# A four-layer graph-attention kernel: preparation of the next steps regrouped, statistics moved earlier, and elu's minimum fused with its scaling

## The chip, the cores and the metric

The kernel runs on one core of one Trainium2 chip. The metric is the device time of one execution in microseconds (us). The engines are TensorE (PE in the profile; PEld is its weight load), VectorE (DVE), ScalarE (ACT), GpSimd (POOL) and SyncE (SP), which here only issues DMAs. Each engine works off its own queue in program order, so an instruction that waits holds up everything behind it on that engine.

## The reference

Sixteen graphs of 1024 nodes with 256 features share one adjacency matrix. Four graph-attention layers follow each other, each with a pre-norm and a residual:

```python
h = jnp.maximum(_layernorm(x, axis=-1), 0.0)
x = x + _L0_gnn_ref(h, adj, L0_gnn_W, L0_gnn_a)   # 4 heads of 64, elu
...
x = x + _L1_gnn_ref(h, adj, L1_gnn_W, L1_gnn_a)   # 1 head of 256, elu
...
x = x + _L2_gnn_ref(h, adj, L2_gnn_W, L2_gnn_a)   # 4 heads of 64, elu
...
x = x + _L3_gnn_ref(h, adj, L3_gnn_W, L3_gnn_a)   # 1 head of 256, relu
```

A layer projects (`q = h @ W`), forms `e[i, j] = leaky_relu(src[i] + dst[j])` for each head, masks it by the adjacency, takes the softmax over j, multiplies by q, and applies elu (`max(y, exp(min(y, 0)) - 1)`) or, in the last layer, relu. Everything is fp32.

## The kernel before

**Steps and slots.** One step is one layer of one graph; there are 64. Four graphs are in flight, and `order_of_steps` interleaves them so that in the long middle part a four-head step (layers 0 and 2) and a one-head step (layers 1 and 3) alternate. Step n has eight *slots*, 8n to 8n+7. In each slot TensorE aggregates one group (L336, matmuls at L348): in a four-head step half of the rows of one head, so that two slots share a head, with matmuls of 64 output columns; in a one-head step an eighth of the rows, with matmuls of 128 columns. ScalarE evicts the group (`y`, L363).

**Weights.** For each head DVE makes eight tiles `w` (L332) of 128x1024, one for each block of 128 source nodes, from a broadcast row `g` that ScalarE has put into PSUM (L327) out of a row that a DMA fetched (L321). A group reads all eight tiles of its head. There are `WBUFS = 18` buffers for these tiles. `emit_tiles` (L456) issues up to 6 tiles a slot in a four-head step and 3 in a one-head step, never more than 18 past the last head that is done. So a four-head step can start with 18 of its 32 tiles made; the nineteenth takes the place of a tile of its first head, which is free when the second group has read it.

**Preparation.** While step n-2 runs, the next steps are prepared in *pieces* (L209): `stats` (eight `bn_stats` on DVE, L221, then ten small POOL operations, L242 to L254), two `normalise` (four ScalarE activations each, L260), and for each half two `transpose` (four PE transposes and one ScalarE eviction each, L268 and L269) and four `project` (two matmuls and a ScalarE eviction each, L279 and L281). The last projection of a half adds two exponentials on ScalarE (L287, L289) and one product on POOL (L291). Then come `factors` (two activations, L297 and L298), `rows` (one transpose, an eviction and a DMA, L303 to L307, then the fetches of L321) and an empty piece that marks the step as prepared. Transposes and projections share two PSUM buffers (`ps_p`), so the third of them waits for ScalarE to have evicted the first.

The lists at L44 to L48 say in which slot, counted from 8(n-2), each piece of step n is issued: `ONE` for one-head steps, `FOUR` for four-head steps, `SOON` and `LATE` where a graph is not free in time. Slots below 0 lie in step n-3, those above 7 in step n-1. `prepare` (L433) issues what is due after the group of each slot. With `FOUR` and `ONE` as they stand, a four-head step of the middle part has PE pieces after seven of its eight groups: slots 0 and 1 with the end of a one-head step's preparation, 0 to 5 and 7 with a four-head step's own. I call a run of such work between two groups a *PE piece*.

**The end of a step.** `finish` (L365) runs in the first slots of the next step: `divide` (reciprocal, L380), `scaled` for each half (y times 1/sum, L386, and for elu `min(y, 0)` into `e`, L391), `exponential` (L395), `add` (`max(e - 1, y)` on DVE, L401, and the residual on POOL, L402; in the last layer one DVE operation, L404). In a four-head step's finish the first half of y is scaled on DVE, the second on POOL; both minima run on POOL. The list `at` (L414) gives the slots: 0, 0, 0, 0, 1, 1, 1 after a four-head step, 0, 0, 1, 1, 2, 2, 3 after a one-head step.

**Pairs.** In what follows a *pair* is a one-head step and the four-head step behind it. There are two kinds. In a *layer-1 pair* the one-head step is a layer 1, so that its elu is finished inside the four-head step; in a *layer-3 pair* it is a layer 3, and its relu, its stores and the load of a new graph are.

Of the kernel before, what the change touches and what calls it, by code (L numbers as in the profile page):

```python
# [30 lines left out]
ALU = mybir.AluOpType  # L31
# [3 lines left out]
P = 128  # L35
# [5 lines left out]

FOUR = (-4, -3, -2, -1, 0, 0, 1, 1, 2, 2, 3, 3, 4, 4, 5, 5, 6, 7, 7, 10)  # L44
ONE = (2, 2, 4, 4, 5, 5, 6, 6, 7, 7, 6, 6, 7, 7, 8, 8, 8, 9, 9, 11)
SOON = (0, 0, 1, 2, 3, 3, 4, 4, 5, 5, 5, 5, 6, 6, 7, 7, 8, 9, 9, 11)
FIRST = (-2, -2, -1, -1, 0, 0, 0, 0, 1, 1, 1, 1, 2, 2, 2, 2, 3, 3, 3, 5)
LATE = (0, 0, 1, 1, 2, 2, 3, 3, 3, 3, 3, 3, 4, 4, 4, 4, 5, 6, 6, 8)  # L48


LAYERS = [
# [8 lines left out]
def kernel(ctx: ExitStack, tc: tile.TileContext, x, adj, ws, avs, out):  # L60
    nc = tc.nc
# [3 lines left out]
    HALF = C // 2  # L65
# [34 lines left out]
    L = len(LAYERS)  # L100
    steps = order_of_steps(B, L)
# [107 lines left out]
    def preparation(n):  # L209

        b, l = steps[n]
        H, slope, _, _ = LAYERS[l]
        D = F // H
        st = state[n]

        def stats(half):
            if half == 0:
                st["bn"] = small.tile([P, C, 6], F32, name="bn")
            bn = st["bn"]
            for c in range(half * HALF, (half + 1) * HALF):  # L220
                nc.vector.bn_stats(bn[:, c, :], xs[b][:, c, :])  # L221
            if n == 0:
                q = slice(half * HALF, (half + 1) * HALF)
                if half == 1:
                    combine_end(slice(0, HALF), nc.vector)
                combine(q, nc.vector)
                if half == 1:
                    combine_end(q, nc.vector)
            elif half == 1:
                combine(slice(0, C), nc.gpsimd)  # L230
                combine_end(slice(0, C), nc.gpsimd)

# [23 lines left out]
        def normalise(half):  # L256
            xn = st["xn", half] = prep.tile([P, HALF, F], F32, name="xn")
            for q in range(HALF):
                c = half * HALF + q
                nc.scalar.activation(xn[:, q, :], xs[b][:, c, :], AF.Identity,  # L260
                                     bias=st["shift"][:, c:c + 1], scale=st["rstd"][:, c:c + 1])
# [44 lines left out]
            st["grow"] = dram.tile([H, C, P], F32, name="grow")  # L306
            nc.sync.dma_start(out=st["grow"].rearrange("h c i -> c h i"), in_=gT)  # L307

        out = [lambda: stats(0), lambda: stats(1), lambda: normalise(0), lambda: normalise(1)]
        for half in range(2):  # L310
            out += [lambda half=half, k=k: transpose(half, k) for k in range(K)]
            out += [lambda c=c: project(c) for c in range(half * HALF, (half + 1) * HALF)]
# [52 lines left out]
    def finish(n):  # L365

        b, l = steps[n]
        H = LAYERS[l][0]
        D = F // H
        st = state[n]  # L370

        def views(half):
            s = slice(half * HALF, (half + 1) * HALF)
            return (xs[b][:, s, :].rearrange("p c (h d) -> p (c h) d", h=H),
                    st["y"][:, s, :, 0:D].rearrange("p c h d -> p (c h) d"),
                    st["r"][:, s, :].rearrange("p c h -> p (c h)"))

        def divide():
            st["r"] = small.tile([P, C, H], F32, name="r")
            nc.vector.reciprocal(st["r"], st["y"][:, :, :, D])  # L380

        def scaled(half):
            xh, yh, r = views(half)

            engine = nc.vector if H > 1 and half == 0 else nc.gpsimd
            engine.tensor_tensor(yh, yh, r[:, :, None].to_broadcast([P, HALF * H, D]),  # L386
                                 op=ALU.mult)
            if l < L - 1:

                e = st["e", half] = prep.tile([P, HALF * H, D], F32, name="e")  # L390
                nc.gpsimd.tensor_scalar(e, yh, 0.0, -3.0e38, op0=ALU.min, op1=ALU.max)  # L391

        def exponential(half):
            if l < L - 1:
                nc.scalar.activation(st["e", half], st["e", half], AF.Exp)  # L395

        def add(half):
            xh, yh, r = views(half)
            if l < L - 1:
                e = st["e", half]  # L400
                nc.vector.scalar_tensor_tensor(e, e, -1.0, yh, op0=ALU.add, op1=ALU.max)  # L401
                nc.gpsimd.tensor_add(xh, xh, e)  # L402
# [12 lines left out]
        return list(zip(at, (divide, lambda: scaled(0), lambda: exponential(0), lambda: scaled(1),  # L415
                             lambda: exponential(1), lambda: add(0), lambda: add(1)))) + (
                    [(4, lambda: store(0)), (4, lambda: store(1))] if l == L - 1 else [])

# [55 lines left out]
    last, agenda_of = {}, []  # L474
    for n, (b, l) in enumerate(steps):

        free = 8 * (last[b % STREAMS] + 1) + (8 if l == 0 else 2) if b % STREAMS in last else -99
        last[b % STREAMS] = n
        start = 8 * (n - 2)
        kind = ONE if LAYERS[l][0] == 1 else SOON if n < 4 else FOUR  # L480
        if free > start + kind[0]:
            kind = LATE
            start = max(free, agenda_of[-1][0] + 5)
        agenda_of.append([start + k for k in kind] if n > 1 else FIRST)
        if n > 2:

            was = agenda_of[n - 1]
            assert agenda_of[n][2] >= was[4] and agenda_of[n][3] >= was[10]
    ending = []
    later = {}  # L490
    with tc.manual_schedule():
        blocks = [mask_rows(c) for c in range(C)]
        layer = [weight_columns(l) for l in range(L)]
        layer[0][0](nc.scalar)
        load(0, 2)
        load_weights(0)
        for c in range(C):
            blocks[c][0]()
        load(1)
        load_weights(1)  # L500
# [12 lines left out]

        for i in (0, 1, 2, 3):
            first[i]()
        layer[0][2]()
        first[4]()
        first[5]()
        layer[0][3]()
        sign(0)  # L520
        for i, c in ((6, 1), (8, 2), (10, 3), (12, 4), (14, 5)):
            first[i]()
            first[i + 1]()
            sign(c)
        for piece in first[16:]:
# [12 lines left out]
        blocks[6][4]()  # L538
        blocks[7][4]()
        prepare(-1)  # L540
        for i in range(2, STREAMS):
            load_weights(i)
            load(i)

        for l, at in ((1, 1), (2, 8 * 3 + 3), (3, 8 * 5 + 3)):
            for i, piece in zip((0, 1, 2, 8), layer[l]):
                later[at + i] = piece
        for n in range(len(steps)):
            for k, (h, i0, per) in enumerate(groups(n)):
# [52 lines left out]
```

## Time and profile before

| what | value |
|---|---|
| median of 3 runs | 2643.99 us (2643.78 to 2644.14) |
| the profiled execution | 2644.88 us |
| its span, first to last instruction | 2643.1 us |
| PE busy | 2543.8 us (96%), granted clock 0.992 |
| DVE busy | 1987.4 us (75%) |
| ACT busy | 1141.3 us (43%) |
| POOL busy | 1014.6 us (38%) |
| a layer-1 pair, from row transpose to row transpose (L303) | 80.47 us |
| a layer-3 pair, likewise | 79.7 us |

The span is what the engines' instructions cover; the execution's own time has 1.8 us around it. The timeline of an engine lists its instructions in order, equal ones merged: start, time until the last of them ends, engine, line, operation, output and inputs, count, and in brackets the idle time before it and what ended that. An fp32 matmul shows as two records. Since matmuls are pipelined, what a stretch of them costs is best read as the distance from its start to the next start.

### The profile page before, as it was taken

The numbers are of one execution on the slowest core, as the hardware profiler recorded it, in microseconds if no ns is written. First come the engines' busy times: TensorE is split into PE (matmuls) and PEld (weight loads), VectorE is DVE, ScalarE is ACT, GpSimd is POOL, SyncE is SP. The second block draws the span as 40 slices with busy tenths as digits, with TensorE's granted clock in tenths as the row PEclk, the third lists the DMA queues.
The fourth block names the chain that finished last, engine by engine and source line by source line (L and its number), as shares of the span: only waits on it lengthen the run. The fifth ranks groups of instructions, "written<-read, shape, count | busy, mean of one in ns | idle before, by whom it ended". The sixth has DMA issues, their size and how long they took to land.

```text
span 2643.1 us, 87745 instructions
## 1 busy us (share of the span) xinstructions
PE 2543.8 (96%) x40088; PEld 2252.3 (85%) x40088; DVE 1987.4 (75%) x2112; ACT 1141.3 (43%) x2502; POOL 1014.6 (38%) x1072
## 2 busy tenths in 40 slices
PE   6889999999999999999999999999999999999999
PEld 4778888888888888888888888888888888888888
DVE  7887667877877777777778777778778777777873
ACT  4443444444444344444344444444443444444341
POOL 2233454432343443533332544443433334444231
PEclk8999999999999999999999999999999999999999
DMA  4101011121111110111211111101112201101101
GB/s 176 51 26 42 10 42 34 42 74 54 62 50 58 42 35 18 42 42 66 74 58 58 42 34 42 42 27 58 50 58 74 74 16 36 42 34 42 51 18 56
DMA packets 36987, 128.98 MB, mean 49 GB/s; under 512 B 6278, under 2 KB 9094, under 8 KB 34696
## 3 DMA queue, kind: packets, MB, share of 16 engines
q1 hardware_dynamic: 36606, 123.36, 13.4%
q8 instruction: 314, 5.14, 0.8%
q14 instruction: 57, 0.47, 0.1%
q10 hardware_dynamic: 10, 0.00, 0.0%
HBM read 105.91 MB, written 17.43 MB: 47 GB/s over the span
## 4 chain that ended last, share of the span: by engine, by line
PE 88%; DVE 6%; ACT 4%; issue 1%; POOL 1%; DMA 0%; POOLq 0%; DVEq 0%
PE acc L348 67%; PE pp L279 16%; PE pp L268 5%; DVE w L332 4%; ACT xn L260 2%; ACT e L395 1%; DVE bn L221 1%; PE pp L303 0%; ACT y L363 0%; ACT whx L281 0%; DVE e L401 0%; POOL shift L254 0%; DVE mask L194 0%; POOL e L391 0%; DMA x<-in_x 0%
## 5 line engine op out<-in xcount | busy, mean ns | idle before, releaser
L348 PE MATMUL acc<-whx,w 128*64 128x65 f32 x36864 | 1924.4, 241 | 21.2 <-DVE w L332 14.8
L348 PEld LDWEIGHTS acc<-whx,w 128*64 128x64 f32 x36864 | 1753.6, 144 | 195.6 <-issue 58.7
L332 DVE SCALAR_TENSOR_TENSOR w<-g,rcol,mask 128x1024 f32<-128x1024 f32 x1280 | 1547.2, 1273 | 232.7 <-PE acc L348 146.7
L363 ACT ACTIVATE y<-acc 128x260 f32<-128x260 f32 (+1 forms) x504 | 193.7, 384 | 1059.4 <-PE acc L348 1059.4
L291 POOL TENSOR_TENSOR whx<-whx 128x1024 f32<-128x1024 f32 x128 | 256.5, 2004 | 834.9 <-ACT whx L289 783.4
L279 PE MATMUL pp<-wx,hT 128*128 128x264 f32 (+1 forms) x2048 | 514.0, 393 | 40.3 <-ACT whx L281 32.3
L279 PEld LDWEIGHTS pp<-wx,hT 128*128 128x128 f32 x2048 | 373.2, 190 | 118.5 <-ACT whx L281 43.1
L260 ACT ACTIVATE xn<-x,shift,rstd 128x256 f32<-128x256 f32 x512 | 261.7, 588 | 123.2 <-POOL shift L254 121.2
L281 ACT ACTIVATE whx<-pp 128x264 f32<-128x264 f32 (+1 forms) x512 | 194.0, 385 | 232.8 <-PE pp L279 232.5
L402 POOL TENSOR_TENSOR x<-x,e 128x1024 f32<-128x1024 f32 x96 | 227.7, 2373 | 141.8 <-DVE e L401 139.5
L401 DVE SCALAR_TENSOR_TENSOR e<-e,y 128x1024 f32<-128x1024 f32 x96 | 145.4, 1515 | 181.0 <-ACT e L395 181.0
L391 POOL TENSOR_SCALAR e<-y 128x1024 f32<-128x1024 f32 x96 | 127.2, 1325 | 205.7 <-DVE y L386 192.0
L221 DVE BATCH_NORM_STATS2 bn<-x 128x6 f32<-128x256 f32 x512 | 178.0, 409 | 33.2 <-POOL x L402 30.0
L386 POOL TENSOR_TENSOR y<-y,r 128x1024 f32<-128x1024 f32 x94 | 178.1, 1896 | 33.6 <-DVE r L380 33.6
L327 ACT ACTIVATE g<-gs 128x1024 f32<-128x1024 f32 x160 | 163.5, 1023 | 6.8 <-DVE w L332 6.2
L268 PE MATMUL pp<-ident,xn 128*128 128x128 f32 x1024 | 152.0, 281 | 13.8 <-ACT whx L281 5.9
L268 PEld LDWEIGHTS pp<-ident,xn 128*128 128x128 f32 x1024 | 117.1, 142 | 44.9 <-ACT whx L281 23.2
L269 ACT ACTIVATE hT<-pp 128x512 f32<-128x512 f32 x256 | 141.0, 588 | 10.5 <-PE pp L268 5.4
L242 POOL TENSOR_TENSOR dev<-bn 128x8 f32<-128x8 f32 x63 | 13.2, 209 | 334.2 <-DVE bn L221 334.2
L380 DVE RECIPROCAL r<-y 128x32 f32<-128x32 f32 (+1 forms) x63 | 17.6, 279 | 158.8 <-ACT y L363 158.8
L248 POOL TENSOR_TENSOR rstd<-rstd,neghalf 128x8 f32<-128x8 f32 (+1 forms) x65 | 107.0, 1647 | 12.5 <-DVE shift L249 7.6
L395 ACT ACTIVATE e<-e 128x1024 f32<-128x1024 f32 x96 | 100.7, 1049 | 18.6 <-POOL e L391 18.6
(63 smaller groups left out, 436.7 us busy)
## 6 DMA issues: line engine op xcount, KB each, us to landing
gs<-grow SPq DMA_DIRECT2D x160, 512.0 KB
x<-in_x SPq DMA_DIRECT2D x15, 1024.0 KB
out<-x SPq DMA_DIRECT2D x30, 512.0 KB
w<-in_adj SPq DMA_DIRECT2D x8, 512.0 KB
x<-in_x SPq DMA_DIRECT2D x2, 512.0 KB
wx<-in_L_gnn_W SPq DMA_DIRECT2D x8, 128.0 KB
out<-x SPq DMA_DIRECT2D x8, 128.0 KB
grow<-gT SPq DMA_DIRECT2D x32, 16.0 KB
```

What stands on the lines that cost most here:

```text
L221: nc.vector.bn_stats(bn[:, c, :], xs[b][:, c, :])
L260: nc.scalar.activation(xn[:, q, :], xs[b][:, c, :], AF.Identity, bias=st["shift"][:, c:c + 1], scale=st["rstd"][:, c:c + 1])
L268: nc.tensor.transpose(pt[:, q, :], st["xn", half][:, q, k * P:(k + 1) * P], ident)
L279: nc.tensor.matmul(pw, lhsT=st["hT", half][:, k, q * P:(q + 1) * P], rhs=wx[l][:, k, :], start=(k == 0), stop=(k == K - 1))
L281: nc.scalar.activation(st["whx"][:, c, :], pw, AF.Copy)
L291: nc.gpsimd.tensor_tensor(wh[:, :, :, 0:D], wh[:, :, :, 0:D], wh[:, :, :, D:D + 1].to_broadcast([P, HALF, H, D]), op=ALU.mult)
L327: nc.scalar.activation(g, state[n]["gs", h], AF.Copy)
L332: nc.vector.scalar_tensor_tensor(w, state[n]["g", h], state[n]["rcol"][:, jc, h:h + 1], masks[LAYERS[steps[n][1]][3]][:, jc, :], op0=ALU.m ...
L348: nc.tensor.matmul(acc[o % P:o % P + cols, q, :], lhsT=st["w", h, jc][:, o:o + cols], rhs=st["whx"][:, jc, h * (D + 1):(h + 1) * (D + 1)], ...
L363: nc.scalar.activation(st["y"][:, i0:i0 + per, h, :], acc, AF.Copy)
L386: engine.tensor_tensor(yh, yh, r[:, :, None].to_broadcast([P, HALF * H, D]), op=ALU.mult)
L402: nc.gpsimd.tensor_add(xh, xh, e)
```

## The change

It has four parts.

- **Order of the preparation.** In a four-head step of the middle part only slots 0 and 2 are followed by PE pieces. Slot 0 takes the last four projections of a one-head step (before: two in the slot ahead and two here) together with the first four projections and the second pair of transposes of the next four-head step; slot 2 takes the row transpose of the one-head step and the last four projections of that four-head step. The first pair of transposes goes to the last slot of the one-head step ahead, and the row transpose to slot 0 of the one-head step behind.
- **Statistics.** The small POOL operations become a piece of their own (`combine_all`). Both `stats` pieces of a four-head step move to slot 0 of the one-head step ahead (from its slots 4 and 5), the combination to slot 3, and the two `normalise` to slots 5 and 6 (from 6 and 7).
- **elu after a four-head step.** DVE computes `e = min(y, 0) * r` in one operation for both halves, and POOL does both products `y * r`. Before, DVE did one product, POOL the other and the two minima. After a one-head step the operations stay as they were.
- **Bookkeeping.** `scaled(1)` is issued ahead of `exponential(0)`; a late preparation may start up to three slots earlier, which makes steps 7 and 9 `LATE` and changes the start of step 60; steps are entered into the agenda one ahead.

```diff
-FOUR = (-4, -3, -2, -1, 0, 0, 1, 1, 2, 2, 3, 3, 4, 4, 5, 5, 6, 7, 7, 10)
-ONE = (2, 2, 4, 4, 5, 5, 6, 6, 7, 7, 6, 6, 7, 7, 8, 8, 8, 9, 9, 11)
...
+FOUR = (-8, -8, -5, -3, -2, -1, -1, 0, 0, 0, 0, 0, 0, 2, 2, 2, 2, 3, 8, 8, 10)
+ONE = (2, 2, 2, 4, 4, 5, 5, 6, 6, 6, 6, 6, 6, 8, 8, 8, 8, 8, 10, 10, 12)
...
+LATE = (0, 0, 0, 1, 1, 2, 2, 3, 3, 3, 3, 3, 3, 4, 4, 4, 4, 5, 6, 6, 8)
...
-            elif half == 1:
+
+        def combine_all():
+            if n > 0:
                 combine(slice(0, C), nc.gpsimd)
                 combine_end(slice(0, C), nc.gpsimd)
...
-        out = [lambda: stats(0), lambda: stats(1), lambda: normalise(0), lambda: normalise(1)]
+        out = [lambda: stats(0), lambda: stats(1), combine_all, lambda: normalise(0), lambda: normalise(1)]
...
         def scaled(half):
             xh, yh, r = views(half)
-
-            engine = nc.vector if H > 1 and half == 0 else nc.gpsimd
-            engine.tensor_tensor(yh, yh, r[:, :, None].to_broadcast([P, HALF * H, D]),
-                                 op=ALU.mult)
+            rb = r[:, :, None].to_broadcast([P, HALF * H, D])
             if l < L - 1:
 
                 e = st["e", half] = prep.tile([P, HALF * H, D], F32, name="e")
+                if H > 1:
+                    nc.vector.scalar_tensor_tensor(e, yh, 0.0, rb, op0=ALU.min, op1=ALU.mult)
+            nc.gpsimd.tensor_tensor(yh, yh, rb, op=ALU.mult)
+            if l < L - 1 and H == 1:
                 nc.gpsimd.tensor_scalar(e, yh, 0.0, -3.0e38, op0=ALU.min, op1=ALU.max)
...
-        return list(zip(at, (divide, lambda: scaled(0), lambda: exponential(0), lambda: scaled(1),
+        return list(zip(at, (divide, lambda: scaled(0), lambda: scaled(1), lambda: exponential(0),
                              lambda: exponential(1), lambda: add(0), lambda: add(1)))) + (
...
-            start = max(free, agenda_of[-1][0] + 5)
+            start = max(free, agenda_of[-1][0] + 5, start - LATE[7])
...
-                while planned < len(steps) and agenda_of[planned][0] <= 8 * n + k:
+                while planned < len(steps) and min(
+                        a[0] for a in agenda_of[planned:planned + 2]) <= 8 * n + k:
```

More of the change, by code (lines that the diff above doesn't have):

```diff
@@ L39 @@
 WBUFS = 18
-FOUR = (-4, -3, -2, -1, 0, 0, 1, 1, 2, 2, 3, 3, 4, 4, 5, 5, 6, 7, 7, 10)
-ONE = (2, 2, 4, 4, 5, 5, 6, 6, 7, 7, 6, 6, 7, 7, 8, 8, 8, 9, 9, 11)
-SOON = (0, 0, 1, 2, 3, 3, 4, 4, 5, 5, 5, 5, 6, 6, 7, 7, 8, 9, 9, 11)
-FIRST = (-2, -2, -1, -1, 0, 0, 0, 0, 1, 1, 1, 1, 2, 2, 2, 2, 3, 3, 3, 5)
-LATE = (0, 0, 1, 1, 2, 2, 3, 3, 3, 3, 3, 3, 4, 4, 4, 4, 5, 6, 6, 8)
+FOUR = (-8, -8, -5, -3, -2, -1, -1, 0, 0, 0, 0, 0, 0, 2, 2, 2, 2, 3, 8, 8, 10)
+ONE = (2, 2, 2, 4, 4, 5, 5, 6, 6, 6, 6, 6, 6, 8, 8, 8, 8, 8, 10, 10, 12)
+SOON = (0, 0, 0, 1, 2, 3, 3, 4, 4, 5, 5, 5, 5, 6, 6, 7, 7, 8, 9, 9, 11)
+FIRST = (-2, -2, -2, -1, -1, 0, 0, 0, 0, 1, 1, 1, 1, 2, 2, 2, 2, 3, 3, 3, 5)
+LATE = (0, 0, 0, 1, 1, 2, 2, 3, 3, 3, 3, 3, 3, 4, 4, 4, 4, 5, 6, 6, 8)
 LAYERS = [
@@ L482 @@
             kind = LATE
-            start = max(free, agenda_of[-1][0] + 5)
+            start = max(free, agenda_of[-1][0] + 5, start - LATE[7])
         agenda_of.append([start + k for k in kind] if n > 1 else FIRST)
         if n > 2:
+            assert agenda_of[n][7] >= 8 * (n - 2)
             was = agenda_of[n - 1]
-            assert agenda_of[n][2] >= was[4] and agenda_of[n][3] >= was[10]
+            assert agenda_of[n][3] >= was[5] and agenda_of[n][4] >= was[11]
     ending = []
@@ L512, in sign @@
                 blocks[c - 1][3]()
-        for i in (0, 1, 2, 3):
+        for i in (0, 1, 3, 4):
             first[i]()
         layer[0][2]()
-        first[4]()
         first[5]()
+        first[6]()
         layer[0][3]()
         sign(0)
-        for i, c in ((6, 1), (8, 2), (10, 3), (12, 4), (14, 5)):
+        for i, c in ((7, 1), (9, 2), (11, 3), (13, 4), (15, 5)):
             first[i]()
@@ L524 @@
             sign(c)
-        for piece in first[16:]:
+        for piece in first[17:]:
             piece()
```

## The prediction

> **What bounds it now.** I read the page first, then the timelines of PE, DVE, ACT and POOL over one pair in the middle (1055 to 1137 us), then the distances between row transposes over the whole span. The page's chain of work that ended last is PE:
>
> ```profile
> PE 88%; DVE 6%; ACT 4%; issue 1%; POOL 1%; DMA 0%; POOLq 0%; DVEq 0%
> ```
>
> DVE, busy for 75%, is second, so the question is what PE loses and whether DVE lets it have that back. PE at the end of the one-head step and in the four-head step behind it:
>
> ```profile
> 1086.99 1.91 PE L279 MATMUL pp<-wx,hT 128*128 128x258 f32 x8
> 1090.17 2.01 PE L279 MATMUL pp<-wx,hT 128*128 128x258 f32 x8 [1.27 <-ACT whx L281]
> 1092.11 3.95 PE L348 MATMUL acc<-whx,w 128*64 128x65 f32 x128
> 1095.99 2.01 PE L279 MATMUL pp<-wx,hT 128*128 128x258 f32 x8
> 1097.84 1.29 PE L268 MATMUL pp<-ident,xn 128*128 128x128 f32 x8
> 1099.07 3.95 PE L348 MATMUL acc<-whx,w 128*64 128x65 f32 x128
> ...
> 1109.57 2.05 PE L279 MATMUL pp<-wx,hT 128*128 128x264 f32 x8
> 1111.55 3.95 PE L348 MATMUL acc<-whx,w 128*64 128x65 f32 x128
> ...
> 1128.17 7.69 PE L348 MATMUL acc<-whx,w 128*64 128x65 f32 x256
> 1135.79 0.28 PE L303 MATMUL pp<-ident,gcol 128*32 128x128 f32 x1
> ```
>
> One group alone takes 3.88 us (1092.11 to 1095.99), two in a row 7.62 (1128.17 to 1135.79): 3.74 each and 0.14 for each uninterrupted block. Two projections take 1.98 here (1109.57 to 1111.55) and 1.74 in the one-head step (1080.64 to 1082.38; at 264 columns 1.78 by width), so a piece costs another 0.20. Each interruption of the 64-column work thus costs 0.34 us. The bracket is a stall: ScalarE's `xn` for the four-head step began only at 1087.51, after 3.19 us of waiting for POOL's `shift`, and the eviction behind it was late. The Trainium skill, "TensorEngine Tiling (Array Packing)", section Key Properties, says that a change of tiling mode drains TensorE; it gives no price, the 0.34 is this trace's.
>
> DVE in the same four-head step:
>
> ```profile
> 1102.25 7.24 DVE L332 SCALAR_TENSOR_TENSOR w<-g,rcol,mask 128x1024 f32<-128x1024 f32 x6 [4.26 <-PE acc L348]
> 1109.41 1.22 DVE L401 SCALAR_TENSOR_TENSOR e<-e,y 128x1024 f32<-128x1024 f32 x1
> 1110.54 2.47 DVE L332 SCALAR_TENSOR_TENSOR w<-g,rcol,mask 128x1024 f32<-128x1024 f32 x2
> 1112.93 1.24 DVE L401 SCALAR_TENSOR_TENSOR e<-e,y 128x1024 f32<-128x1024 f32 x1
> 1114.73 9.63 DVE L332 SCALAR_TENSOR_TENSOR w<-g,rcol,mask 128x1024 f32<-128x1024 f32 x8 [0.56 <-PE acc L348]
> 1125.49 7.24 DVE L332 SCALAR_TENSOR_TENSOR w<-g,rcol,mask 128x1024 f32<-128x1024 f32 x6 [1.14 <-PE acc L348]
> 1136.33 0.35 DVE L380 RECIPROCAL r<-y 128x32 f32<-128x32 f32 x1 [3.59 <-ACT y L363]
> ```
>
> It stands idle until the second group frees the first buffers (4.26 us), then makes 22 tiles and two adds, is done at 1132.7, and waits 3.59 us for the step to end. Those 3.59 us are what the change will draw on.
>
> **Part 1, PE alone.** Four-head step now 43.80 us (1092.11 to 1135.91), seven blocks. After: three blocks, 8 x 3.74 + 3 x 0.14 = 30.34. Piece after slot 0: today's (two projections and transposes, 1095.99 to 1099.07) 3.08, two more projections 1.74, four of 264 columns 3.56, and a new stall of 0.33: between the last one-head projection and the next there are four small activations on ScalarE, which take 1.49 us from eviction to eviction today (1098.04 to 1099.53), so the third of the following projections finds its PSUM buffer free 2.11 us after they begin instead of 1.78. Sum 8.71. Piece after slot 2: today's row transpose and two projections with their stall, 2.73 (1102.95 to 1105.68), and 1.78: 4.51; in a layer-3 pair, without the exponential ahead of it, 1.99 (1183.41 to 1185.40) and 1.78: 3.77. The step is 43.56 or 42.82. One-head step now 36.67 (1055.44 to 1092.11). After: eight groups at 3.475 (20.85 for six) 27.80, rows 0.12, first transposes 0.87, four projections and transposes 2.88 + 1.74 = 4.62, the moved transposes 1.02 (as 1115.43 to 1116.45): 34.43. The stall of 1.27, with 0.17 around it, goes: the statistics come five slots earlier, so `shift` is no longer what `xn` waits for. A pair falls from 80.47 to 77.99, or from 79.72 to 77.25: **2.48 us each**.
>
> **Part 2, what DVE returns.** Times from the start of the new four-head step. Its second group begins at 3.88 + 8.71 = 12.59, not 6.96; the first buffer is free 3.18 later as today (1099.07 to 1102.25), at 15.77. With all 18 buffers full, DVE can do nothing earlier; its two adds stand behind six of the waiting tiles. Six tiles at 1.195 to 22.93, add 1.13, two tiles to 26.45, add to 27.6; the next buffers come free 3.18 after the fourth group's start (24.72), at 27.90; fourteen tiles to 44.63. The step ends at 43.56: DVE is **1.07 us late** into the one-head step. In a layer-3 pair the second add meets POOL's `whx` product (about 25.3 to 27.2) and ends at 28.2, so DVE is done at 44.93 against 42.82: **2.11 late**. The tiles themselves still arrive: the first one-head group needs its eighth 3.04 us after its start. But the elu chain stands behind them on DVE.
>
> The chain in the one-head step, from the moment D at which DVE is free: reciprocal 0.38, two fused minima at 1.14, eight `bn_stats` of the other graph 2.62 (today they come later): D+5.28. The nearest row for a fused minimum is L386's 1.23 us product with the same broadcast; L401's contended 2.06 bounds it above. POOL's two products (1.90 each) begin when the second minimum ends its reading and hold until D+6.4. Then the first add; it and the second end by D+8.5, POOL's two x adds (2.36 each) at D+13.3; statistics of the second half and the combination 1.48 and 4.22 (1068.48 to 1069.96 to 1074.18): `xn` starts at D+18.95. From `xn` to the next group are 2.82 us at least (140.31 to 143.13, where PE waits for each `xn`). So the seventh group starts at D+21.77; by PE alone it would at 0.12 + 20.85 + 0.87 = 21.84. Today it starts at 21.72 with `xn` at 18.74: the chain has 0.16 to spare, hence the loss is about D: 1.0 and 2.0 us.
>
> That DVE and POOL exclude each other is seen here:
>
> ```profile
> 1062.57 2.36 POOL L402 TENSOR_TENSOR x<-x,e 128x1024 f32<-128x1024 f32 x1
> ```
> ```profile
> 1063.95 2.06 DVE L401 SCALAR_TENSOR_TENSOR e<-e,y 128x1024 f32<-128x1024 f32 x1 [2.25 <-ACT e L395]
> ```
>
> The add took 2.06 instead of 1.23 us, ending about 1.07 after POOL did. `bn_stats` beside the same kind of POOL operation is not slowed (four in 1.39). The skill agrees ("SBUF — State Buffer", section SBUF: two separate sides: an exclusive lock for the whole instruction, held by whoever starts first). A rule that speaks against moving the minima is in "GPSIMD Engine Reference", section Engine selection: one-input operations run at roughly line rate on GpSimd. Here POOL's minimum took 1.04 us, less than the 1.23 that DVE pays; by that rule alone the move only loads DVE, 1.14 us a pair, which is inside the chain above.
>
> **Other parts.** POOL loses 2 x 1.04 us and gains 1.90 a pair, neither on a path but the chain's. SP: the rows DMA of a four-head step moves one slot back, behind group and exponential, some 5 us later; today's fetches were issued 3 us after it (1055.99, 1057.85) and the first `g` is not wanted before 10.9 us: hidden; uncovered it would hold ScalarE about 1 us. Stores and load in a layer-3 pair follow the adds, about 3 us later; the load landed about 13 us before the step's end: hidden. The `at` order and the DVE minimum let ScalarE's first exponential go about 1.2 us sooner in the four-head steps at the start (it waited 7.78 and 6.06 us for POOL `e` there), while DVE, which bounds those, gets 1.14 more in four places: -2.4 to +4.6, taken as 0. Steps 7, 9, 60 (`LATE`) and the pairs before 414 and after 2417 us keep more pieces: -3 to +3, taken as 0.
>
> **Sum.** From 414.5 to 2417.25 us there are 25 pairs, 13 with 80.47 and 12 with 79.7. 13 x (2.48 - 1.0) + 12 x (2.48 - 2.0) = 19.2 + 5.8 = 25.0. The span falls from 2643.1 to 2618.1; the execution has 1.8 more, and was 0.9 above the median, so against the median: 2643.99 - 25.0 = **2619.0**.
>
> **Rivals.**
> 1. The chain doesn't bind: DVE gets through sooner, or POOL's products come between other work. For it: 1 us is little against a chain of 22 us. Against: 22 tiles and two adds from 15.77 can't end before 44.3. The price is Part 1 whole, 25 x 2.48 = 62: 2582.
> 2. Everything is given back. If POOL takes the port between the two minima (its product is ready just as DVE turns to the second), the second ends 1.9 later and the chain is 0.95 longer: 25 x 0.95 = 24, giving 2643. Also here: the pieces are as they say, but 0.34 is an artefact of modelled matmul ends.
> 3. **Slower:** PE waits for `w`. Place: first group of the one-head step. Price: one us per us beyond D = 3.04, on top of a chain that then stalls by 3. At D = 4 a pair loses 4.0 - 2.48 = 1.5: 2644 + 38 = 2682; the change turns slower from D = 2.5 on. Fused minima at 2.06 and port losses of both adds would bring 1 to 2 us. Against: the first minimum finds POOL idle.
>
> **Chances.** Forecast 0.54 (2605 to 2636), rival 1 0.19, rival 2 0.14, rival 3 0.13. Leaving out the slow rival, the range is 2578 to 2646; the forecast's own is 2605 to 2636. A measurement of this kernel tells about 0.2% (5 us) from no change: faster 0.73, same 0.14, slower 0.13.
>
> **What would show it.** Right: two PE pieces in a four-head step, pairs of about 79.0 and 79.2 us, no 1.27 stall, DVE idle some 9.5 us ahead of the nineteenth tile, reciprocal 1 to 2 us after the step's end, PE transposes waiting for `xn` at slot 5 of the one-head step. Wrong: no such wait and pairs of 77 to 78; or PE idle behind `w`.

## The result, and the profile after

The changed kernel takes 2641.12 us (median of 4 runs, 2640.89 to 2642.87) beside 2643.93 for the kernel before (4 runs): a ratio of 0.9991, 95% interval 0.9973 to 1.0008. That is no difference that this measurement can tell. I had forecast 2619.0, with a range of 2578 to 2646 in all and of 2605 to 2636 for the forecast's own mechanism. The profiled execution took 2640.99, its span is 2639.2 us.

On the page after, DVE is busy for 77% (75), ACT and POOL hardly changed. The line of the chain that ended last answers to the first line shown of before, where PE had 88% and DVE 6%:

```profile
PE 66%; DVE 17%; POOL 7%; ACT 6%; issue 3%; DMA 0%; DVEq 0%; ACTq 0%
```

So PE now waits for chains on other engines in much of the span. PE's timeline of the changed kernel, at the end of a one-head step (layer 1) and in the four-head step behind it, answers to the rows of before:

```profile
1081.09 0.76 PE L271 MATMUL pp<-ident,xn 128*128 128x128 f32 x5 [0.17 <-ACT xn L263]
...
1098.11 5.54 PE L282 MATMUL pp<-wx,hT 128*128 128x258 f32 x24
...
1106.93 7.69 PE L351 MATMUL acc<-whx,w 128*64 128x65 f32 x256
1114.55 0.27 PE L306 MATMUL pp<-ident,gcol 128*8 128x128 f32 x1
...
1119.06 21.25 PE L351 MATMUL acc<-whx,w 128*64 128x65 f32 x650
```

There are two PE pieces, as forecast: 8.82 us from 1098.11 to 1106.93 (forecast 8.71) and 4.51 from 1114.55 to 1119.06 (forecast 4.51). The stall of 1.27 is gone; in its place the transposes ahead of 1081.69 wait for `xn` (1.92 us from 1079.77, where they took 0.87 before). DVE over the same stretch:

```profile
1059.76 0.34 DVE L383 RECIPROCAL r<-y 128x32 f32<-128x32 f32 x1
1060.21 2.36 DVE L392 SCALAR_TENSOR_TENSOR e<-y,r 128x1024 f32<-128x1024 f32 x2
...
1110.11 7.24 DVE L335 SCALAR_TENSOR_TENSOR w<-g,rcol,mask 128x1024 f32<-128x1024 f32 x6 [9.99 <-PE acc L351]
...
1122.24 16.78 DVE L335 SCALAR_TENSOR_TENSOR w<-g,rcol,mask 128x1024 f32<-128x1024 f32 x14 [0.21 <-PE acc L351]
1138.94 0.34 DVE L383 RECIPROCAL r<-y 128x32 f32<-128x32 f32 x1
```

The idle time ahead of the nineteenth tile is 9.99 us (4.26 before). After it DVE never pauses for more than 0.21 us (the rows left out are two tiles and the two adds, without a wait), and it is late: the reciprocal, which had waited 3.59 us, now waits for nothing and starts 0.94 us after the step's last eviction of `y` began (1058.82). In the kernel before it was 0.42 us, the eviction itself taking 0.39. All this is as forecast. The pairs are 79.18 us (80.47 before) in layer 1 and 79.06 (79.7) in layer 3; forecast were 79.0 and 79.2.

The loss lies elsewhere. A ruler that shows it is the start of each step's last `y` eviction; its distances are the steps' lengths (us, from the profiled executions):

| steps | before | after |
|---|---|---|
| 0 to 5, sum to the end of 5 | 334.45 | 328.00 |
| 6 (one head) | 33.74 | 40.39 |
| 7 | 46.42 | 45.11 |
| 8 (one head) | 34.05 | 46.82 |
| 9 to 55, sum | 1888.23 | 1865.85 |
| 56 to 59, sum | 157.69 | 161.68 |
| 60 (four heads) | 46.24 | 50.78 |
| 61 and 62, sum | 70.22 | 68.70 |

The pairs in the middle gain 22.4 us and the start 6.45. Steps 6 to 8 give 18.1 back, steps 56 to 60 give 8.5. This is step 8 of the changed kernel, on DVE, then on ScalarE, then on PE (the last `y` eviction of step 7 began at 413.50):

```profile
414.85 7.24 DVE L335 SCALAR_TENSOR_TENSOR w<-g,rcol,mask 128x1024 f32<-128x1024 f32 x6 [1.38 <-ACT g L330]
422.01 0.34 DVE L383 RECIPROCAL r<-y 128x32 f32<-128x32 f32 x1
```
```profile
443.52 4.04 ACT L263 ACTIVATE xn<-x,shift,rstd 128x256 f32<-128x256 f32 x8 [10.78 <-POOL shift L257]
```
```profile
444.18 2.81 PE L271 MATMUL pp<-ident,xn 128*128 128x128 f32 x8 [8.38 <-ACT xn L263]
```

Six tiles `w` of step 9 stand on DVE ahead of the reciprocal that ends step 7. Here the reciprocal comes 8.5 us after the eviction began; in the kernel before it came 0.42 us after it (414.62):

```profile
415.04 0.35 DVE L380 RECIPROCAL r<-y 128x32 f32<-128x32 f32 x1 [3.59 <-ACT y L363]
```

The elu, the statistics and `xn` follow it, and PE stands idle for 8.38 us. That is not the whole loss of 12.8 us in this step. Late in the idle time the granted clock fell to half, and the eight transposes took 2.59 us (0.87 before), the group behind them 5.26 (3.48 before). This row of a table of stretches shows the transposes; its figures are the stretch, its length, busy time and count of PE, PEld, DVE, ACT and POOL, PE's clock, the DMA engines' busy share and GB/s:

```profile
444.00:446.70 2.70, 2.48 (x8) 1.60 (x9) 0.00 (x0) 2.70 (x7) 2.36 (x5) 0.50 0.00 0
```

The code says why. With `FOUR` beginning at -8 the graphs of steps 7, 9 and 60 are not free in time, so their lists become `LATE`, which no step of the kernel before used. (Ahead of the prediction I put this down to late preparations being allowed an earlier start; that only moves the start of step 60.) The last number of a list is the empty piece that marks a step as prepared, and only then may `emit_tiles` go on to its tiles. `FOUR` sets the mark at 10 (slot 2 of step n-1), behind `finish`. `LATE` sets it at 8 from its start, which for steps 7 and 9 is slot 7 of step n-2: the tiles of step 9 are issued before the `finish` of step 7.

### The profile page after: what moved, and what is told of

It reads as the page before. It is cut to its first block, busy times and chain, and to the rows that moved or that the text cites. A ratio compares the mean times of both kernels' runs of the same rounds, so it can differ in the third digit from the quotient of the medians.

```text
span 2639.2 us, 87794 instructions
## 1 busy us (share of the span) xinstructions
PE 2539.8 (96%) x40088; PEld 2256.5 (86%) x40088; DVE 2041.7 (77%) x2144; ACT 1133.4 (43%) x2502; POOL 1021.5 (39%) x1040
## 3 DMA queue, kind: packets, MB, share of 16 engines
q1 hardware_dynamic: 36606, 123.36, 13.3%
q8 instruction: 314, 5.14, 0.8%
## 4 chain that ended last, share of the span: by engine, by line
PE 66%; DVE 17%; POOL 7%; ACT 6%; issue 3%; DMA 0%; DVEq 0%; ACTq 0%
PE acc L351 46%; PE pp L282 15%; DVE w L335 10%; PE pp L271 4%; POOL x L406 3%; DVE e L405 3%; DVE bn L222 2%; ACT xn L263 2%; POOL rstd L251 2%; ACT e L399 1%; DVE e L392 1%; ACT whx L284 1%; ACT rcol L290 0%; ACT gcol L301 0%; ACT whx L292 0%
## 5 line engine op out<-in xcount | busy, mean ns | idle before, releaser
L282 PE MATMUL pp<-wx,hT 128*128 128x264 f32 (+1 forms) x2048 | 488.6, 390 | 18.8 <-ACT whx L284 11.2
L393 POOL TENSOR_TENSOR y<-y,r 128x1024 f32<-128x1024 f32 x126 | 264.3, 2108 | 618.7 <-DVE e L392 490.8
L282 PEld LDWEIGHTS pp<-wx,hT 128*128 128x128 f32 x2048 | 379.6, 191 | 98.7 <-ACT whx L284 23.5
L406 POOL TENSOR_TENSOR x<-x,e 128x1024 f32<-128x1024 f32 x96 | 238.1, 2486 | 161.0 <-DVE e L405 155.5
L405 DVE SCALAR_TENSOR_TENSOR e<-e,y 128x1024 f32<-128x1024 f32 x96 | 175.6, 1839 | 41.7 <-ACT e L399 35.5
L271 PE MATMUL pp<-ident,xn 128*128 128x128 f32 x1024 | 168.6, 284 | 32.1 <-ACT xn L263 28.4
L392 DVE SCALAR_TENSOR_TENSOR e<-y,r 128x1024 f32<-128x1024 f32 x64 | 75.5, 1221 | 2.2
L408 DVE SCALAR_TENSOR_TENSOR x<-y,x 128x1024 f32<-128x1024 f32 x30 | 43.3, 1444 | 10.0 <-POOL y L393 10.0
```

Source lines behind the costliest of these rows:

```text
L271: nc.tensor.transpose(pt[:, q, :], st["xn", half][:, q, k * P:(k + 1) * P], ident)
L282: nc.tensor.matmul(pw, lhsT=st["hT", half][:, k, q * P:(q + 1) * P], rhs=wx[l][:, k, :], start=(k == 0), stop=(k == K - 1))
L393: nc.gpsimd.tensor_tensor(yh, yh, rb, op=ALU.mult)
```

## Experiments

Theory A: the pairs do what was forecast, and the early mark of `LATE` eats the gain. Rivals: the lateness of those pieces themselves, or the new elu operations, everywhere a little. Each series was timed beside the kernel before on its own chip (2644.38 to 2645.66 us there, so times of different series compare to about 2 us); ratios are to that, with 95% intervals.

**1. The mark alone.** Only the last number of `LATE` differs from the changed kernel.

```diff
-LATE = (0, 0, 0, 1, 1, 2, 2, 3, 3, 3, 3, 3, 3, 4, 4, 4, 4, 5, 6, 6, 8)
+LATE = (0, 0, 0, 1, 1, 2, 2, 3, 3, 3, 3, 3, 3, 4, 4, 4, 4, 5, 6, 6, 11)
```

> The changed kernel with one number different: the last, empty piece of LATE, which marks a step as prepared, moves from 8 to 11, where FOUR has it; all other pieces stay. Theory A (in steps 6 and 8 the early mark of steps 7 and 9 lets DVE issue six weight tiles of the next four-head step ahead of the elu of the step just ended, so that normalisation starts late and PE waits for xn): step 8 falls from 46.8 to about 35 us and step 6 from 40.4 to about 35, time about 2624 us. Rival B (LATE puts the statistics and both normalisations into the wrong slots): steps 6 and 8 stay as they are, time about 2641 us.

Measured: 2623.23 us, 0.9916 (0.9902 to 0.9931). Steps 6, 7 and 8 are 35.46, 45.11 and 34.14: 17.6 of the 18.1 us are back. DVE at the same place of this kernel, where step 7 ends at 407.09:

```profile
407.51 0.35 DVE L383 RECIPROCAL r<-y 128x32 f32<-128x32 f32 x1 [0.46 <-ACT y L366]
```

The pieces are as late as in the changed kernel, only the tiles come behind the `finish`. Theory A holds, and in this stretch the granted clock stays at 1.00. Step 60 stays at 50.80, so the loss at the end is not the mark's.

**2. The same three steps without `LATE`.** They keep `FOUR`, with their statistics at -6.

```diff
+        if kind is FOUR and start + FOUR[0] < free <= start + FOUR[2] - 1:
+            kind = (FOUR[2] - 1, FOUR[2] - 1) + FOUR[2:]
         if free > start + kind[0]:
```

> The changed kernel with steps 7, 9 and 60 on FOUR again, only their two statistics pieces at -6 instead of -8, since their graphs are not free earlier. Theory A: as e1 within 3 us, about 2624, with at most a few us more from the end of the kernel (step 60). Rival B: clearly faster than e1, by the 18 us that steps 6 and 8 lost, and e1 unchanged.

Measured: 2632.85 us, 0.9953 (0.9937 to 0.9970): 10 us above run 1, a miss. Step 8 is 34.66 as expected, but step 4 takes 49.30 instead of 44.31 and step 6 38.64 instead of 35.46. Slot -6 of step 7 lies in step 4, which has four heads and is bound by DVE. There DVE's timeline shows sixteen statistics at once; behind them PE waits for `w` five times in a row from 270.2 us on, 0.7 to 0.9 us each:

```profile
259.75 5.31 DVE L222 BATCH_NORM_STATS2 bn<-x 128x6 f32<-128x256 f32 x16
```

The run confirms the place of the loss and shows that the early statistics have a price where the step that takes them has four heads. Step 60 takes 52.10 without `LATE`, so its loss doesn't come from that list.

**3. The earlier elu in the changed kernel.** Both minima return to POOL, the first product to DVE, in the earlier order.

```diff
+            engine = nc.vector if H > 1 and half == 0 else nc.gpsimd
+            engine.tensor_tensor(yh, yh, r[:, :, None].to_broadcast([P, HALF * H, D]),
+                                 op=ALU.mult)
...
-                if H > 1:
-                    nc.vector.scalar_tensor_tensor(e, yh, 0.0, rb, op0=ALU.min, op1=ALU.mult)
-            nc.gpsimd.tensor_tensor(yh, yh, rb, op=ALU.mult)
-            if l < L - 1 and H == 1:
                 nc.gpsimd.tensor_scalar(e, yh, 0.0, -3.0e38, op0=ALU.min, op1=ALU.max)
...
```

> The changed kernel with the elu of before (DVE scales the first half, POOL the second, POOL does both minima). Theory C (the chain of elu, statistics and normalisation in the one-head step sets the pair): the chain is about 0.7 us shorter with the old operations, since POOL does not hold the port for two products ahead of the first add; pairs about 78.5 us instead of 79.2, time about 2624 us. Rival D (the fused minimum shortens the chain, as it takes the minimum off POOL): pairs longer than 79.2, time above 2645 us.

Measured: 2625.54 us, 0.9926 (0.9912 to 0.9941). The one-head steps fall from 34.65 to 33.72 after layer-1 pairs' four-head steps and from 35.28 to 34.69 after the others; step 60 rises from 50.78 to 54.04. Theory C holds, with 0.93 and 0.59 us a pair instead of 0.7. DVE is as late as in the changed kernel (0.95 us in layer 1, 1.94 in layer 3): what has become shorter is the chain from the reciprocal to `xn`, 18.26 us instead of 19.20 in layer 1.

**4. Mark and earlier elu together** (the edits of 1 and 3).

> The changed kernel with LATE's mark at slot 11 and the earlier division of elu (both minima on POOL, first product on DVE). Theory C (each us that the two fused minima add to DVE between reciprocal and statistics comes back on PE in the one-head step): 0.93 us for each of 13 one-head steps after layer 1 and 0.6 for each of 12 after layer 3, 19 us in all, less some 3 us more in step 60: 2623.2 - 16 = 2607 us. Rival (the 15.6 us that this edit brought alone came mostly from steps 6 and 8, which the mark has already mended): 2618 to 2623.

Measured: 2608.50 us, 0.9864 (0.9850 to 0.9879): 14.7 below run 1. The gains of the two edits add up to within 1 us, so the two losses are independent.

**5. The new elu alone, in the kernel before.**

> The kernel before with only the new elu: its minimum fused with the scaling on DVE, both products on POOL, in the new order of pieces; the preparation stays in its seven pieces. With the old agenda the statistics come after the elu chain has ended and DVE has 3.59 us to spare at the end of the four-head step, but xn waits for shift behind it (1.27 us of PE's time in each pair). Theory C: the chain is 0.9 us longer, and the stall of 1.27 grows by as much: 25 pairs, 2644 + 20 = 2664 us at most. Rival (the statistics, five slots later than in the changed kernel, have room for it): 2640 to 2648.

Measured: 2661.43 us, 1.0062 (1.0045 to 1.0079), so slower, if only by 0.6%. A pair loses 0.9 us, as theory C has it, though DVE is not late at all here (the reciprocal still waits 3.59 us for the eviction). PE's timeline in the one-head step:

```profile
1080.58 0.76 PE L268 MATMUL pp<-ident,xn 128*128 128x128 f32 x3
1081.50 0.77 PE L268 MATMUL pp<-ident,xn 128*128 128x128 f32 x5 [0.16 <-ACT xn L260]
...
1095.35 2.01 PE L279 MATMUL pp<-wx,hT 128*128 128x258 f32 x8 [1.51 <-ACT whx L281]
```

From 1080.58 to the next group (1082.10) are 1.52 us, where before the transposes took 0.87 (1156.76 to 1157.63), and the stall has grown from 1.27 to 1.51: 0.89 together, and the one-head step grew by 0.89 (34.05 to 34.94). So of the change's parts, the new elu costs 15 to 16 us in either agenda (runs 3 and 5), and the agenda with the earlier elu brings 20 (run 3), or 37 with the mark mended (run 4).

**6. One buffer of `w` fewer**, with run 1's mark.

```diff
-WBUFS = 18
+WBUFS = 17
```

> The changed kernel with LATE's mark at 11 and one buffer of w fewer (17). Theory D (what DVE is late by at the end of the four-head step is what a pair loses: it stands idle until the second group frees the first buffers, and one tile more is left to make after that, 1.19 us): the reciprocal comes 2.2 us after the step's end in layer 1 and 3.3 in layer 3, each pair is 1.2 us longer, 25 x 1.2 = 30 us: 2653 (in layer 3 some more, where the first group waits for its eighth tile). Rival (the 0.6 to 1.2 us that one-head steps lost is due to POOL's lock or to the pieces themselves): within 5 us of 2623.

Measured: 2665.42 us, 1.0079 (1.0062 to 1.0096), 42 above run 1. In layer 1 the reciprocal comes 2.14 us after the step's end (1059.10 against 1056.96), as expected, and the one-head step is 0.9 longer, not 1.2. In layer 3 a pair is 1.2 to 2.9 longer. There the reciprocal comes 2.49 us after the step's end, less than the 3.3 expected. The rival is refuted. By the ruler, steps 9 to 56 take 29.9 us more than in run 1, which is the 30 of theory D, though not as 1.2 in every pair; the other 10 us of the profiled executions lie ahead of step 9 (6.6) and behind step 56 (3.8).

**7. Pieces after slots 1 and 3.** If DVE is late because the first buffers come free after piece A, then the first head should be done before it.

```diff
-FOUR = (-8, -8, -5, -3, -2, -1, -1, 0, 0, 0, 0, 0, 0, 2, 2, 2, 2, 3, 8, 8, 10)
-ONE = (2, 2, 2, 4, 4, 5, 5, 6, 6, 6, 6, 6, 6, 8, 8, 8, 8, 8, 10, 10, 12)
+FOUR = (-8, -8, -5, -3, -2, -1, -1, 1, 1, 1, 1, 1, 1, 3, 3, 3, 3, 4, 8, 8, 10)
+ONE = (2, 2, 2, 4, 4, 5, 5, 6, 6, 6, 6, 6, 6, 9, 9, 9, 9, 9, 11, 11, 12)
```

> The changed kernel with the two long pieces of the four-head step one slot later, after slots 1 and 3 instead of 0 and 2, so that a head's two groups are not parted. Theory E (the long piece between the two groups of the first head holds DVE's buffers and makes DVE late into the one-head step by 1.0 to 2.1 us, and PE then waits as long for xn): DVE waits about 1 us instead of 10 for the nineteenth tile, is done before the step's end, the wait for xn falls from 1.1 to 0.3 us, pairs about 78.2 and 77.6 us, time about 2621 us. Rival (DVE's lateness does not matter, the chain in the one-head step is long by itself): pairs stay at 79.2 and 79.0, time about 2641 us.

Measured: 2627.44 us, 0.9932 (0.9918 to 0.9947). Layer-1 pairs fall to 77.97 as expected, and step 60 to 46.16, so the loss there came from the place of the pieces: in the changed kernel a projection during step 60 waited 3.74 us for an eviction that stood on ScalarE behind an exponential, and that behind DVE's minima. But the four-head steps of layer-3 pairs take 45.0 to 47.7 us, where most of them took 43.78, which nothing of mine had foreseen.

**8. Mark and odd slots together** (the edits of 1 and 7).

> Both earlier edits to the changed kernel together: LATE's mark at slot 11, and FOUR's two pieces after slots 1 and 3 (ONE's after 1 and 3 of the next four-head step with it). Theory A (the mark and the place of the pieces are independent losses): step 8 falls from 46.6 to 34.1 us and step 6 from 40.1 to 35.5, 17 us less than the 2627.4 of the pieces alone: 2610 us. Theory B (with the pieces later, DVE's run-ahead is no longer what step 8 waits for): within 4 us of 2627.

Measured: 2610.59 us, 0.9872 (0.9858 to 0.9887). Theory A holds again. The new loss in layer-3 pairs stays. This is PE, then SP of this kernel in such a step:

```profile
784.78 4.42 PE L351 MATMUL acc<-whx,w 128*64 128x65 f32 x144
790.59 14.65 PE L351 MATMUL acc<-whx,w 128*64 128x65 f32 x384 [1.39 <-issue]
```
```profile
782.95 0.32 SPq L324 DMA_DIRECT2D gs<-grow  x1
783.37 0.85 SPq L411 DMA_DIRECT2D out<-x  x2
```

The 144 records of matmuls are the first group of a head, 128, which has read all eight of that head's tiles, and 16 of its second group, which reads the same tiles, so PE has no operand to wait for; and "issue" means that the profile knows no releaser. The table of stretches of this kernel, with the figures in the same order as above, shows what happens just ahead of it:

```profile
784.00:786.00 2.00, 2.00 (x45) 1.60 (x45) 2.00 (x2) 1.43 (x4) 0.00 (x0) 1.00 0.96 229
786.00:788.00 2.00, 2.00 (x76) 2.00 (x74) 1.55 (x2) 0.00 (x0) 1.90 (x1) 1.00 0.99 391
788.00:790.00 2.00, 1.20 (x42) 1.11 (x39) 0.00 (x0) 1.19 (x4) 0.00 (x0) 1.00 0.39 150
```

The fetch of `g` (0.5 MB) and two stores (0.5 MB each) are issued within 1.3 us and fill the DMA engines to 96 and 99 per cent; then PE starves. In the kernel with pieces after slots 0 and 2 the second store waits for its `add` and goes some 4 us after the first. The page's list of queues has one for instructions:

```profile
q8 instruction: 314, 5.14, 0.8%
```

Its 5.14 MB in 314 packets are 16.4 KB each, and 64 bytes for each of the 80,176 matmul and weight-load records of PE. (The list doesn't say whose code it is; the 64 bytes are an estimate that gives it all to PE.) A group of 64-column matmuls has 128 of each: 256 x 64 bytes are one such packet in 3.74 us. A group of the one-head step has 16 of each.

The DMA records show the fetch itself. In the view of 780 to 788 us this queue doesn't appear: its last packet had landed at 779.36. In the view of 788 to 790 us it has one:

```profile
q8 instruction: 1, 0.02, 2.9%
```

It starts at 788.37, as the burst ends, and lands at 789.31; PE, idle since 789.20, goes on at 790.59, which is 1.28 us later. All 21 waits of this kind in run 8 end 1.2 to 1.6 us after such a packet has landed.

**9. The same kernel with its transfers apart.** The stores go ahead of the fetch on SP's queue, the load from ScalarE's queue two slots later.

```diff
-            if half == 1 and b + STREAMS < B:
-                load(b + STREAMS)
...
+        def reload():
+            if b + STREAMS < B:
+                load(b + STREAMS, engine=nc.scalar)
...
-                    [(4, lambda: store(0)), (4, lambda: store(1))] if l == L - 1 else [])
+                    [(2, lambda: store(0)), (2, lambda: store(1)), (6, reload)] if l == L - 1 else [])
```

> As the run before (mark at 11, pieces after slots 1 and 3), but the two stores of a finished graph stand ahead of the fetch of g on SP's queue (slot 2 instead of 4), and the load of the next graph goes from ScalarE's queue at slot 6, so that no stretch has two stores and a fetch at once. Theory S (in the four-head steps after layer 3 PE starves for 1 to 2 us without a releaser, because its instructions are fetched by the same DMA engines, which are 95 to 98 per cent busy in the 5 us before): the idle time of 1.4 to 2.0 us put down to issue goes, these steps fall from 45.0-47.7 to about 43.1-43.8 us, and the time is 15 to 25 us below the run before: about 2590. Theory G (PE waits there because g, and so w, comes 3.1 us late): the steps stay at 45 to 47 us, and the time within 4 us of the run before.

Measured: 2583.81 us, 0.9768 (0.9754 to 0.9783), 26.8 below run 8. All but four of the waits put down to issue are gone, and those four lie in the first 270 and the last 180 us. PE's waits on issue fell as these rows of the two kernels' lists of waits show (sum, count, longest), run 8 first:

```profile
PE acc L351 <- issue: 24.4, 21, 2.0
```
```profile
PE acc L351 <- issue: 2.2, 4, 0.8
```

All the four-head steps in layer-3 pairs take 43.78 to 43.88 us. DVE waits for `g` as long as in run 8 (3.12 us there too, until 790.67), in the same place:

```profile
783.12 9.63 DVE L335 SCALAR_TENSOR_TENSOR w<-g,rcol,mask 128x1024 f32<-128x1024 f32 x8 [3.12 <-ACT g L330]
```

So theory G falls and theory S stands; the packets shown under run 8 are the direct evidence for it. The Trainium skill, "Runtime: NRT & Kernel Launch", section Instruction fetch mechanics, says that the sequencer fetches its code by a DMA queue in blocks of 16 KiB and that this is mostly hidden; the packets agree with the 16.4 KB here, and the waits of up to 2.0 us show where it isn't hidden.

**10. Smaller stores in run 8's places.** This separates the traffic from the order of the queues.

```diff
-                out=out[b].rearrange("(p c) f -> p c f", p=P)[:, half * HALF:(half + 1) * HALF],
-                in_=xs[b][:, half * HALF:(half + 1) * HALF, :])
+                out=out[b].rearrange("(p c) f -> p c f", p=P)[:, half * HALF:half * HALF + 1],
+                in_=xs[b][:, half * HALF:half * HALF + 1, :])
```

> The kernel with the mark at 11 and pieces after slots 1 and 3 (2610.6 us), with stores that write one of four row blocks of each half; three quarters of the output are left out. Stores, fetch and load keep their places and queues. Theory S (PE starves because the transfers occupy the DMA engines that bring its instructions): with 0.25 MB stored in place of 1 MB, the idle time put down to issue in the four-head steps after layer 3 goes, and the time is 15 to 27 us below: 2584 to 2596. Rival (what helped was that the load left SP's queue, or the order of SP's queue): 2605 to 2611.

Measured: 2594.25 us, 0.9814 (0.9798 to 0.9830): the queues' order is the same, three quarters of the stored bytes are gone, and some 16 of run 9's 27 us with them. What is left stands behind the load of 1 MB, which now goes earlier (782.38 us here, 791.46 in run 8). This is the place that answers to the one shown for run 8:

```profile
784.00:786.00 2.00, 2.00 (x77) 2.00 (x72) 1.91 (x2) 0.06 (x1) 0.00 (x0) 1.00 0.84 344
786.00:788.00 2.00, 0.57 (x19) 0.43 (x15) 2.00 (x3) 0.39 (x1) 0.00 (x0) 1.00 0.29 111
```

This step is 47.80 us long, 4.0 more than in run 9. PE's wait is 2.0 of it, and it ends 1.37 us after an instruction packet has landed (787.19); behind it the granted clock was 0.50 from 790 to 792 us and 0.74 from 792 to 794.

**11. Run 9 with the earlier elu** (the edit of 3 added).

> The fastest kernel so far (mark at 11, pieces after slots 1 and 3, stores ahead of the fetch, load from ScalarE's queue) with the earlier division of elu. Theory C (the minima on DVE cost only where DVE comes late into the one-head step; with the later pieces it no longer does): nothing in the 25 pairs, between -2 and +1 us in each of steps 1, 2, 58 and 60: 2580 to 2588 against 2583.8. Rival (the minima cost 0.9 and 0.6 us a pair wherever DVE stands): 2565.

Measured: 2578.34 us, 0.9747 (0.9732 to 0.9761). Between the two, and both theories fail in their wording. The one-head steps still fall, from 34.15 to 33.60 and from 34.07 to 33.60, though DVE is no longer late: in run 9 the reciprocal starts at 1026.66, 0.42 us after the last eviction began (1026.24), as in the kernel before. So theory C's condition is refuted, and the minima cost something wherever DVE stands, as the rival has it, only 0.5 us a pair instead of 0.9 and 0.6. The chain from the reciprocal to `xn` is 19.23 us in run 9 and 18.31 here (layer 1); steps 9 to 56 gain 12.4 us. But the start loses 7.4: step 2 takes 49.95 instead of 44.95, step 5 47.70 instead of 44.22.

**12. Each elu where it is shorter**: the fused minimum in steps 1, 2, 4, 57, 59 and 60, the earlier form elsewhere. (The expectation names the first five; the condition takes in step 60 as well.)

```diff
+        fused = H > 1 and (0 < n < 7 or n > 56)
...
```

> As the kernel with the mark at 11, pieces after slots 1 and 3, moved stores and the earlier division of elu (2578.3 us), but elu's minimum fused on DVE in the steps of the start and the end alone (steps 1, 2, 4, 57, 59), where by the distances between y evictions the fused form was better: steps 2 and 5 lost 5.0 and 3.5 us with the earlier division, step 60 lost 1.4, while the pairs gained 0.5 each. If the two are independent: 2578.3 - 9 = 2569. Rival (what a start step gains, the next one gives back, as step 4 gave 0.5 here): 2574 to 2578.

Measured: 2569.74 us, 0.9718 (0.9704 to 0.9733), the fastest of all; step 2 is 44.95, step 60 46.16. That is the forecast for two independent gains.

## Why the prediction was wrong

- **What bounds the kernel, and Part 1: right.** The price of an interruption, 0.34 us, gave pieces of 8.71 and 4.51; they measure 8.82 and 4.51. Rival 2's other ground, that the 0.34 is an artefact, is thereby gone. In run 3, where PE's transposes wait for nothing in layer 1, the pair is 78.25 us, against 77.99 for PE alone.
- **Part 2: right in its times, not in what it charges.** DVE late by 1.07 forecast, 0.94 measured in layer 1; 2.11 forecast in layer 3, 1.95 measured (reciprocal at 822.60, step's end at 820.65). `xn` at D+18.95 forecast, D+19.2 measured (1078.96). Rival 1's clause, that the chain doesn't bind, is refuted by the wait for `xn` and by run 6. But "the loss is about D" doesn't hold: with DVE as late and the earlier elu (run 3), PE in layer 1 doesn't wait for `xn` at all. There the loss is the longer chain; in layer 3 the chain is 0.6 us of it.
- **The lock: seen, in another place.** The two minima took 2.36 us together, so POOL's product does not come between them, and rival 2's mechanism did not occur. But the first add took 2.16 us, beside POOL's second product, and the second 3.29, beside POOL's `x` addition, as these rows of the changed kernel show (POOL, then DVE):

```profile
1061.58 4.61 POOL L393 TENSOR_TENSOR y<-y,r 128x1024 f32<-128x1024 f32 x2 [14.64 <-DVE e L392]
1067.36 2.35 POOL L406 TENSOR_TENSOR x<-x,e 128x1024 f32<-128x1024 f32 x1 [1.16 <-DVE e L405]
```
```profile
1065.11 2.16 DVE L405 SCALAR_TENSOR_TENSOR e<-e,y 128x1024 f32<-128x1024 f32 x1
1067.50 3.29 DVE L405 SCALAR_TENSOR_TENSOR e<-e,y 128x1024 f32<-128x1024 f32 x1 [0.22 <-ACT e L399]
```

  POOL was first both times and ended at 1066.19 and 1069.71; each add ended 1.08 later, as in the kernel before. I had both adds done by D+8.5, the second ended at D+11; the chain lost little by it, since POOL's next addition followed at once and ended at D+13.5 (forecast 13.3).
- **The sum over the pairs: right.** 13 x 1.29 + 12 x 0.64 = 24.5 against the forecast 25.0. The ruler shows 22.4 over steps 9 to 55.
- **"Steps 7, 9, 60 (`LATE`) and the pairs before 414 and after 2417 us keep more pieces: -3 to +3, taken as 0": this is the step that failed.** Steps 6 to 8 cost 18.1 us, and steps 56 to 60 8.5, so a term taken as 0 was 26.6. I had noticed that three steps change their list and asked only how many PE pieces they have. What the list's last number releases on DVE I did not ask. By run 1 that number alone is worth 18 us. Of the 8.5 at the end, run 7 gives 4.6 to the place of the pieces in step 60.
- **"start -2.4 to +4.6, taken as 0"**: -6.45 measured, outside the range; 1.3 of it lies in step 0, which differs as much between the changed kernel and run 1. This gain was luck: it hid a quarter of the loss. The fused minima are worth 0.9 to 3.8 us of it in steps 1 to 5 (the changed kernel beside run 3, run 1 beside run 4; 6.3 with the agenda of runs 11 and 12), and I put the rest down to the new agenda without a run that shows it.
- **No rival was right.** Rival 2 gives 2643, near the measured time, by mechanisms that did not occur. Rival 3 (PE waits for `w`) did not occur in the pairs, DVE being less than 3.04 late.
- **What I did not price at all** is the elu by itself: I put its two minima into a chain that I knew to bind, and never worked the chain out with the old operations. They cost 15 us, beside 25 that I forecast for the whole. The chain from the reciprocal to `xn` is 18.3 us with the old operations in every agenda (the kernel before, runs 3 and 11) and 19.2 with the new ones (run 5, the changed kernel, run 9), in layer 1. In the changed kernel POOL's two products stand ahead of the first add, which ends 7.5 us after the reciprocal's start; in run 3 it is 5.8.
- **The sum as measured:** 22.4 in the middle, 6.5 at the start and 1.5 in steps 61 and 62 gained, 18.1 and 8.5 lost, leaves 3.7 of the 3.9 us between the two spans.

What stays open: some 4 us of the loss in steps 56 to 59 (step 57 is 49.28 here, 47.87 with the later pieces), why the dose of run 6 falls so unevenly on the pairs, and what the new agenda alone does in steps 1 to 5.

## What to carry to other kernels

When a change alters a hand-written order, list every step that falls into another branch of the planner, and ask of each of its entries what it releases, above all those that compute nothing: one mark, three slots early, cost 18 us where two dozen regrouped pairs brought 22. An operation that moves onto a chain which ends just as the next stage needs it is paid there, even where its new engine has time to spare ahead of the chain (run 5: 3.59 us to spare, 0.9 lost in each pair); price it by itself, not inside the sum. And a measured "no change" can be two large effects: lengths step by step, side by side, showed in one table what the median hid.

## What the runs showed of the hardware that I had not expected

TensorE can starve for its own code. Where small matmuls need 16.4 KB of instructions in 3.74 us, 4 us of DMA engines at 96 to 99 per cent left PE idle for 1.4 us with no releaser (up to 2.0 elsewhere in run 8), or, in run 10, with a wait put down to a `w` that had been finished at 780.97, 7.6 us before PE went on. Each time PE went on 1.2 to 1.6 us after a packet of 16.4 KB had landed in the queue for instructions. Moving 1 MB of stores by two slots and the load to another queue was worth 26.8 us, more than the change itself was forecast to bring. The kernel before showed 1.0 us of such waits in all (0.4 and 0.6 at 2462 and 2478 us), so its page gave no hint.
